# Four edits to a two-layer vision kernel: mixed channels turned by VectorE in the last half, loads ahead of stores at attention's end, one group loaded tile by tile, attention's last sums on TensorE

## The chip, the cores and the metric

The kernel runs on one core of a Trainium2 chip. A core has a matrix engine (TensorE, "PE" in the profile, with its weight loads as "PEld"), a vector engine (VectorE, "DVE"), an activation engine (ScalarE, "ACT"), a general engine (GpSimd, "POOL"), and a synchronizing engine (SyncE, "SP") that here issues every DMA. The DMAs of one queue are spread over 16 DMA engines. Each engine takes its instructions in program order; they wait for each other through semaphores. TensorE writes into PSUM, a small memory of eight banks; everything else lives in SBUF (128 partitions) or in device memory. The metric is the device time of one execution in microseconds.

## The reference

Input x is (2, 56, 56, 384), fp32. Two layers follow each other. Cut to what matters:

```
# layer 0
h = layer_norm(x); q, k, v = heads(h @ w_qkv + b_qkv)        # 12 heads of 32
scores = q . k over each pixel's 7x7 neighbourhood + rpb
x = x + softmax(scores) v @ w_proj + b_proj
x = x + gelu(layer_norm(x) @ w1 + b1) @ w2 + b2              # 384 -> 1536 -> 384
# layer 1
p = layernorm(x) @ w_in + b_in                               # 384 -> 768
local = depthwise_conv_3x3(p)
mixed = 0.25 * (ema(left-right) + ema(right-left) + ema(top-bottom) + ema(bottom-top)) + local
x = x + layernorm(mixed) @ w_out + b_out                     # norm over 768 channels
x = x + gelu(layernorm(x) @ w1 + b1) @ w2 + b2
```

## The kernel before, in words

There are 6,272 tokens (pixels), or 49 tiles of 128. All is fp32; TensorE runs each fp32 product as two passes, so a product of 3 chunks shows as 6 matmul records. A transpose shows as one.

**Attention.** The image is cut into 14 groups of 8 rows (numbers 0 to 13), a group into 4 windows of 14 columns, a window into 3 units of 4 heads: 168 units, `NU`. The loop at L702 makes one step per unit, with the work of several units in each step, in an order that is written out by hand. At step `s` TensorE computes the scores of unit `s` (L515; where two units fit in one bank, both together), VectorE adds the bias in two halves (`biased`, L530), ScalarE takes the exponential (`numerators`, L536), for unit `s-1` VectorE adds up the 2 or 3 chunks of keys into one tile `sum` (`gathered`, L542 and L544), and for unit `s-2` TensorE multiplies the numerators with the values (L552) and `sum` with a matrix of ones (L558), which gives the softmax denominators. The number of chunks `m` depends on the window: 3 in the middle columns of inner groups, 2 at the edges and in the last group. Once a window has its three units, VectorE turns the denominators (`gather`, L482), inverts them (`invert`) and divides (`divide`, L498 and L500).

Beside that, each step may hold a job for TensorE: queries, keys and values of later groups, or `project` (L573), the output projection of one token tile. VectorE then adds the residual `xr` (L585), to which GpSimd has added the bias (`add_bias`, L571). A residual tile is loaded by `load_residual` (L563), which also sets a countdown: after so many steps GpSimd adds the bias, or when the projection needs it, whichever is first. `END` is `ng - 2`, so groups 12 and 13 are the last two: there no later group is prepared any more. At `s == NU` (L736) the memory of keys and biases is freed, the residuals of the last four tiles are loaded and then the first two groups of the attention's output (`xa`, L742, from `x1f`). The stores of finished tiles are issued at the start of each step (`store_all`, L704), and a further residual load (L706) waits until the store of the tile whose buffer it takes has landed. After the loop (L808) come the additions that are left (`take`), the statistics and inverse deviation of the first group (`norm_of`, `close`), its normalization, and the last projections.

**Two passes.** `passes` (L960) then runs over the tokens in groups of 2 or 3 or 4 tiles (`groups`): layer 0's MLP, then layer 1's input projection. Beside it, `Beside` hands out steps of the convolution and the running averages to VectorE; these go over channels on partitions and are stored to `mix_d`. A second loop (L1428) over `dgroups`, eleven groups of 4 tiles, then 3 and 2, runs layer 1's output projection and MLP. In its iteration `g`:

- the hidden loop, 12 times `hidden` (L1053, matmuls L1047): 3 chunks each
- beside it `measure_beside` for group `g + 1`: the mixed channels `mx` have channels on partitions, but the norm over channels wants tokens on partitions, so `measure` (L1246) turns one tile with six TensorE transposes (L1251) into PSUM, and VectorE takes bn_stats of it there (L214). One tile is taken at m = 3, 5, 7 and 9, for the group `half_way` two steps later; `close` follows, whose power runs on GpSimd (L222)
- `project_out` for group `g + 1`: 6 chunks per row of 128 tokens (L1063, `y<-w_out,mx`), and VectorE scales each row by the inverse deviation and adds the residual (L1272)
- the loads of group `g + 2` (`load_mix`, L1233: `mx` from `mix_d`, and `xa`)
- the MLP's second product, 12 chunks per row (L1063, `y<-w,hid`), output additions (L1447) and stores.

The rows of `project_out` and of the second product share two PSUM buffers, `y`. `half_way` is group 6, the first that reaches into the second image; all of VectorE's mixing has to be done before its load, so that is issued at the end of iteration 4 (L1453), after `beside.until`. The last work of `Beside` is thus finished there.

Of the kernel before, what the change touches and what calls it, by code (L numbers as in the profile page):

```python
# [33 lines left out]
F32 = mybir.dt.float32  # L34
# [6 lines left out]
B, H, W, C = 2, 56, 56, 384  # L41
# [132 lines left out]
def block_kernel(ctx: ExitStack, tc: tile.TileContext, ins: dict, out: bass.AP):  # L174
# [328 lines left out]
    class Unit:  # L503
# [33 lines left out]

        def gathered(self):

            n, t = self.w.keys, lp.tile([P, 4, TT], F32, name="sum", bufs=2)  # L540
            self.sum = t
            nc.vector.tensor_tensor(t[:n], self.pts[:n, :, 0, :], self.pts[:n, :, 1, :], ALU.add)  # L542
            for c in range(2, self.m):
                nc.vector.tensor_tensor(t[:n], t[:n], self.pts[:n, :, c, :], ALU.add)  # L544

        def values(self):

            w, hg, n = self.w, self.hg, self.w.keys
            for c in range(self.m):
                for i in range(4):  # L550
                    h = 4 * hg + i
                    nc.tensor.matmul(  # L552
                        o[i * HD : (i + 1) * HD, hg, :],
                        lhsT=w.vt[:n, c, h * HD : (h + 1) * HD], rhs=self.pts[:n, i, c, :],
                        start=c == 0, stop=c == self.m - 1,
                    )
            for i in range(4):
                nc.tensor.matmul(  # L558
                    sums[i * HD : (i + 1) * HD, hg * TT : (hg + 1) * TT], lhsT=ones_hd[:n, :],
                    rhs=self.sum[:n, i, :], start=True, stop=True,  # L560
                )

    def load_residual(t, pool=lp, bufs=3):  # L563

        xrs[t] = pool.tile([P, C], F32, name="xr", bufs=bufs)
        nc.sync.dma_start(out=xrs[t], in_=xf[t * P : (t + 1) * P, :])
        loaded[t] = 4

    def add_bias(t):
        del loaded[t]  # L570
# [30 lines left out]
    def load_group(src, group, tag):  # L601
        t0, n = group
        t = xp.tile([P, NT, C], F32, name=tag)
        nc.sync.dma_start(
            out=t[:, :n, :], in_=src[t0 : t0 + n * P, :].rearrange("(k p) c -> p k c", p=P)
        )
        return t
# [26 lines left out]
    def store_all():  # L634
        while stores:
            dst, src = stores.pop(0)
            nc.sync.dma_start(out=dst, in_=src)
# [63 lines left out]
    END, THEN = ng - 2, (7, 9, 11, 13, 16, 19, 22)  # L701
    for s in range(NU + 4):  # L702
        n, k, hg, i = s // UG, s % UG, s % NC, s // NC
        store_all()  # L704
        while load:
            load_residual(load.pop(0))  # L706
        if k == 0 and n < ng:
            vals = []
            if n + 1 < ng:
                ahead += [lambda n=n, m=m: query_or_key(n + 1, m, one_bank) for m in range(NC)]  # L710
                vals += tiles_of(n + 1)[2:]
            if n + 2 < ng:
                vals += tiles_of(n + 2)[:2]
            ahead += [lambda t=t: value(t, one_bank) for t in vals]
            if n + 2 < ng:
                ahead += [
                    lambda n=n, m=m: query_or_key(n + 2, m, one_bank) for m in range(NC, 2 * NC)
                ]

            spare = (3, 4, 5) if len(ahead) == 9 else (4, 6)  # L720

        if k == 2 and n + 4 < ng:
            load_x(n + 4)
        if k == 1 and n < ng:
            load_bias(n, NWC - 1)
        if n + 1 < ng and k in (4, 10):
            load_bias(n + 1, 0 if k == 4 else 1)
        if s == NU - UG - 4:
            ectx.close()
            wm = ctx.enter_context(tc.tile_pool(name="w_mlp", bufs=1, side="right"))  # L730
            w1, w2, w_parts = weights(0)
        if s < NU and hg == 2 and s + 1 < NU:
            ws[i + 1] = Window(i + 1)
        if s >= NU - UG - 4 and hg == 2 and w_parts:
            w_parts.pop(0)()
        if s == NU:  # L736
            kctx.close()
            xp = ctx.enter_context(tc.tile_pool(name="x", bufs=2, side="right", reuse_waits="tile"))
            tail_pool = actx.enter_context(tc.tile_pool(name="a_tail", bufs=1))
            for t in range(T2 // P - 4, T2 // P):  # L740
                load_residual(t, tail_pool, 4)
            xs = {g: load_group(x1f, groups[g], "xa") for g in range(2)}  # L742


        if s <= NU:
            for take in taking:
                take()
            taking = []
        if s == NU + 1:
            sctx.close()  # L750
            ps_s = sctx.enter_context(tc.tile_pool(name="a_pss", bufs=4, space=PSUM))
        if s < NU:

            if s not in units:
                units[s] = Unit(ws[i], hg)
                units[s].scores()
                behind = Unit(ws[(s + 1) // NC], (s + 1) % NC) if s + 1 < NU else None
                if behind is not None and (units[s].m + behind.m) * TT <= BANK:
                    behind.scores(units[s].m)
                    units[s + 1] = behind  # L760
        new, before, last = units.get(s), units.get(s - 1), units.pop(s - 2, None)
        done = last.w if last is not None and last.hg == NC - 1 else None
        if last is not None:
            last.values()
        behind = ws.get(i - 1 - (hg == 0))
        if behind is not None and hg == 2:
            behind.invert()
        if behind is not None and hg == 0:
            behind.divide()
            if behind.j == NWC - 1:  # L770
                to_project += tiles_of(behind.n)
            ws.pop(behind.i)
        if n + 3 < ng and k < NT:
            measure_x(n + 3, k)
        for half in range(2):
            if new is not None:
                new.biased(half)
                new.numerators(half)
            if half == 0 and done is not None:
                done.take()  # L780
        if before is not None:
            before.gathered()
        if done is not None:
            done.gather()
        if n < END:
            if ahead and k not in spare:
                taking.append(ahead.pop(0)())
            if to_project and n < END - 1:
                taking.append(project(to_project.pop(0), turning_bank))
        elif ahead:  # L790
            if k != 3:
                taking.append(ahead.pop(0)())
        elif s - END * UG in THEN:
            taking.append(project(to_project.pop(0), one_bank))
        elif s > NU and s < NU + 4 and to_project:
            taking.append(project(to_project.pop(0), any_bank))
        for t in list(loaded):
            loaded[t] -= 1
            if loaded[t] < 0:
                add_bias(t)  # L800
        if n + 3 < ng:
            if k in (4, 5):
                for q in range(2 * k - 8, 2 * k - 6):
                    normalize_x(n + 3, q)
            if k in (8, 9, 11):
                taking.append(channels_of(n + 3, (8, 9, 11).index(k), turning_bank))

    for take in taking:  # L808
        take()
    norm = norm_of(xs[0], groups[0][1], sm)  # L810
    norm.close(groups[0][1])
    norm.shift(groups[0][1])
    xn = normalized(norm, xs[0], groups[0][1])
    for t in to_project:
# [145 lines left out]
    def passes(xs, xn, w1, w2, between=lambda psum: None):  # L960
# [272 lines left out]
        def load_mix(g):  # L1233
            t0, n = dgroups[g]
            mx = io.tile([P, NI, MT], F32, name="mx")
            for b, at, here, n in images(t0, n * P):
                nc.sync.dma_start(
                    out=mx[:, :, here : here + n],
                    in_=mix_d[b][:, :, at : at + n].rearrange("m p t -> p m t"),
                )  # L1240
            x = load_group(x2_d, dgroups[g], "xa")
            if g >= half_way:
                add_row(x, dgroups[g][1], "b_out")
            return mx, x, Norm(sm)
# [9 lines left out]
                parts.append(ps.rearrange("p c q -> p (c q)"))  # L1254
            norm.add(k, parts)

        def measure_beside(m, g, ahead, late=0):

            n = dgroups[g][1]
            k = (m - late) // 2 - 1  # L1260
            if m % 2 == 1 and 0 <= k < n:
                measure(ahead[0], ahead[2], k)
            if m == min(10 + late, NHID - 1):
                ahead[2].close(n)

        def project_out(g, mx, x, inner):
# [161 lines left out]
        for g, (t0, n) in enumerate(dgroups):  # L1428
            hid = []
            for m in range(NHID):  # L1430
                hid.append(hidden(w1, m, hT, n, "L1_conv_b1"))
                if g < last:
                    measure_beside(m, g + 1, ahead, 2 if g + 1 == half_way else 0)
                beside.go(MLP_D)
            res = x3
            if g < last:
# [109 lines left out]
```

## Time and profile before

| | us |
|---|---|
| median of 3 runs | 2710.99 (2710.21 to 2712.02) |
| the profiled execution | 2709.48 |
| its span, first to last instruction | 2707.7 |
| busy: TensorE matmul | 2659.7 (98%) |
| busy: VectorE | 1679.7 (62%) |
| busy: ScalarE | 897.7 (33%) |
| busy: GpSimd | 249.6 (9%) |

A matmul's listed duration holds its way through the array, so neighbours overlap, and listed durations add up to more than the time taken; the distance from start to start is what one costs. A group of the profile is one line of the kernel with its engine, operation and tiles. "A <-B" says that the engine stood idle before A until B. `mm`, `y`, `xi`, `o`, `sums`, `sc` and `tp` are PSUM tiles, the others lie in SBUF; names ending in `_d`, `in_...` and `out` are in device memory.

### The profile page before, as it was taken

How to read it: one execution, taken by the hardware profiler on the slowest of the kernel's cores; microseconds unless marked ns; L12 is line 12 of the kernel's file. 1: busy time of each engine (PE TensorE's matmuls, PEld its weight loads, DVE VectorE, ACT ScalarE, POOL GpSimd, SP SyncE). 2: the span in 40 equal slices, each digit the busy share in tenths (PEclk: the TensorE clock that was granted, in tenths of full speed). 3: DMA queues.
4: the chain of work that ended last, by engine and by line, in shares of the span. 5: the costliest groups of instructions: out<-in, count | busy, mean ns of one | idle time of the engine just before them, and what ended most of it. 6: DMA issues, size and time to landing. Idle time of an engine off the chain costs nothing. (4 is left out here: it accounts for less than half of the span.)

```text
span 2707.7 us, 36333 instructions
## 1 busy us (share of the span) xinstructions
PE 2659.7 (98%) x14975; PEld 1492.9 (55%) x14975; DVE 1679.7 (62%) x2560; ACT 897.7 (33%) x1447; POOL 249.6 (9%) x264
## 2 busy tenths in 40 slices
PE   8999999998899999999999999999999999999998
PEld 4666666655555555555554555555555455555565
DVE  3778877878320188688989888898888522221110
ACT  4555555554222332222344422321233211111111
POOL 1111111111211100000010000000100011110100
PEclk9999999999999999999999999999999999999999
DMA  6423454225410132232354544443354411011000
GB/s 213 133 88 104 150 174 149 77 75 167 135 47 27 64 115 79 104 118 98 120 199 183 206 143 141 164 136 117 142 188 171 153 47 44 12 41 35 30 12 16
DMA packets 131887, 298.91 MB, mean 110 GB/s; under 512 B 10646, under 2 KB 87552, under 8 KB 129408
## 3 DMA queue, kind: packets, MB, share of 16 engines
q1 hardware_dynamic: 131712, 296.50, 31.9%
q8 instruction: 119, 1.95, 0.3%
q14 instruction: 56, 0.46, 0.1%
HBM read 180.86 MB, written 115.61 MB: 109 GB/s over the span
## 5 line engine op out<-in xcount | busy, mean ns | idle before, releaser
L1047 PE MATMUL mm<-hT,w 128*128 128x512 f32 (+2 forms) x1872 | 776.1, 570 | 0.1
L1063 PE MATMUL y<-w,hid 128*128 128x384 f32 x2352 | 764.8, 486 | 0.0
L1063 PEld LDWEIGHTS y<-w,hid 128*128 128x128 f32 x2352 | 445.0, 190 | 305.3 <-issue 0.5
L1047 PEld LDWEIGHTS mm<-hT,w 128*128 128x128 f32 x1872 | 352.1, 191 | 372.8 <-issue 342.4
L1056 ACT ACTIVATE hid<-mm,chan 128x512 f32<-128x512 f32 (+2 forms) x312 | 206.3, 662 | 741.2 <-PE mm L1047 741.2
L1141 DVE SCALAR_TENSOR_TENSOR loc<-pt,taps,loc 128x990 f32<-128x990 f32 (+9 forms) x336 | 377.1, 1122 | 10.0 <-ACT loc L1123 1.7
L536 ACT ACTIVATE pts<-pts 119x448 f32<-119x448 f32 (+3 forms) x336 | 206.5, 642 | 187.9 <-DVE pts L530 187.9
L530 DVE TENSOR_TENSOR pts<-sc,bias 119x448 f32<-119x448 f32 (+3 forms) x336 | 220.8, 699 | 67.7 <-PE sc L515 66.7
L222 POOL TENSOR_TENSOR rs<-rs,mhalf 128x4 f32<-128x4 f32 (+4 forms) x67 | 87.2, 1302 | 1745.6 <-DVE rs L219 1704.1
L386 PE MATMUL ps<-hT,wqkv 128*128 128x448 f32 x504 | 211.9, 559 | 3.5 <-ACT vs L431 1.5
L1047 PE MATMUL mm<-hT,w_in 128*128 128x512 f32 (+2 forms) x468 | 191.7, 568 | 0.6 <-ACT hT L254 0.6
L1063 PE MATMUL y<-w_out,mx 128*128 128x384 f32 x588 | 191.8, 486 | 0.0
L1395 DVE TENSOR_TENSOR xc<-y,xa 128x384 f32<-128x384 f32 x49 | 27.3, 557 | 251.0 <-PE y L1063 250.5
L1447 DVE TENSOR_TENSOR xc<-y,xc 128x384 f32<-128x384 f32 x49 | 27.2, 555 | 218.2 <-PE y L1063 167.8
L1063 PEld LDWEIGHTS y<-w_out,mx 128*128 128x128 f32 x588 | 111.6, 190 | 79.8 <-issue 4.8
L240 ACT ACTIVATE xn<-xc,sh,rs 128x384 f32<-128x384 f32 x98 | 64.7, 698 | 269.3 <-DVE sh L233 269.1
L214 DVE BATCH_NORM_STATS2 st<-xi 128x6 f32<-128x384 f32 x98 | 50.3, 554 | 153.3 <-PE xi L1251 153.2
L1047 PEld LDWEIGHTS mm<-hT,w_in 128*128 128x128 f32 x468 | 88.7, 190 | 101.6 <-issue 91.8
L386 PEld LDWEIGHTS ps<-hT,wqkv 128*128 128x128 f32 x504 | 90.2, 191 | 84.4 <-issue 72.8
L254 ACT ACTIVATE hT<-tp,chan 128x512 f32<-128x512 f32 (+2 forms) x117 | 79.5, 751 | 165.1 <-PE tp L251 165.0
L515 PEld LDWEIGHTS sc<-qT,kT 32*100 32x100 f32 (+3 forms) x3168 | 90.9, 169 | 69.5 <-DVE pts L530 17.3
L515 PE MATMUL sc<-qT,kT 32*100 32x112 f32 (+3 forms) x3168 | 113.8, 270 | 9.0 <-DVE pts L530 8.4
(89 smaller groups left out, 2435.4 us busy)
## 6 DMA issues: line engine op xcount, KB each, us to landing
bias<-in_bias_t SPq DMA_DIRECT2D x16, 1344.0 KB
loc<-loc_d SPq DMA_DIRECT2D x24, 784.0 KB
mixed<-mix_d SPq DMA_DIRECT2D x24, 784.0 KB
mix_d<-mixed SPq DMA_DIRECT2D x24, 784.0 KB
xa<-x_d SPq DMA_DIRECT2D x22, 768.0 KB
p_d<-mx SPq DMA_DIRECT2D x10, 1536.0 KB
mx<-mix_d SPq DMA_DIRECT2D x10, 1536.0 KB
pt<-p_d SPq DMA_DIRECT2D x18, 560.0 KB
```

The costliest lines, as they stand in the source:

```text
L214: nc.vector.bn_stats(st[:n, i, :], x)
L222: nc.gpsimd.tensor_tensor(rs, rs, mhalf[:n, :k], ALU.pow)
L240: nc.scalar.activation(out[:, k, :], x[:, k, :], AF.Identity, bias=self.sh[:n, k : k + 1], scale=self.rs[:n, k : k + 1],)
L254: nc.scalar.activation(dst[:, c, : len(xs) * n], tp, AF.Identity, bias=col(b, c), scale=col(g, c))
L386: nc.tensor.matmul(ps, lhsT=wqkv[:, c, m * P : (m + 1) * P], rhs=hT[:, c, half_of(n)], start=c == 0, stop=c == NC - 1,)
L515: nc.tensor.matmul(sc[i // 2][: w.keys, i % 2, (first + c) * TT : (first + c + 1) * TT], lhsT=kT[d, hg, w.keys_at + r * w.kc : w.keys_at + ...
L530: nc.vector.tensor_tensor(self.of(half), sc[half][:n, :, at].rearrange("p h (c q) -> p h c q", q=TT), self.w.bias[:n, 4 * self.hg + h : 4 ...
L536: nc.scalar.activation(self.of(half), self.of(half), AF.Exp)
L1047: nc.tensor.matmul(ps[:, : n * P], lhsT=w[:, c, m * P : (m + 1) * P], rhs=hT[:, c, : n * P], start=c == 0, stop=c == NC - 1,)
L1056: nc.scalar.activation(t[:, : n * P], ps[:, : n * P], AF.Gelu, bias=col(b1, m))
L1063: nc.tensor.matmul(ps, lhsT=t[:, k * P : (k + 1) * P], rhs=w[:, m, :], start=m == 0, stop=m == len(lhs) - 1,)
L1141: nc.vector.scalar_tensor_tensor(to, pt[:, lo + dy - self.top : hi + dy - self.top, xt : xt + n], self.tap(dy, dx), to, ALU.mult, ALU.add,)
```

## The change

Four things are changed.

1. In attention's last two groups (`w.n >= END`) `gathered` adds nothing; TensorE multiplies every chunk of the numerators with the ones, summing in PSUM.
2. At `s == NU` the block that frees memory and loads is moved ahead of `store_all` and the residual loads, `xa` goes ahead of the last four residuals, and these get a countdown of 2 steps instead of 4. After the loop the first group's statistics and `close` go ahead of the waiting `take`s.
3. The load of `mx` for group `half_way` is cut into tiles of 128 tokens (a tile that lies in both images takes two DMAs), and that group is measured at m = 3, 5, 7, 9 like the others, no longer two steps later.
4. For groups after `half_way`, `measure_by_vector` takes the place of `measure`: 16 VectorE transposes per tile, each of 32 partitions and six blocks of 32 columns, into an SBUF tile, and bn_stats from there. It is called at m = 0, 2, 4, 6.

```
         def gathered(self):
-            n, t = self.w.keys, lp.tile([P, 4, TT], F32, name="sum", bufs=2)
-            self.sum = t
+            n, self.parts = self.w.keys, [self.pts[:, :, c, :] for c in range(self.m)]
+            if self.w.n >= END:
+                return
+            t = lp.tile([P, 4, TT], F32, name="sum", bufs=2)
+            self.parts = [t]
             nc.vector.tensor_tensor(t[:n], self.pts[:n, :, 0, :], self.pts[:n, :, 1, :], ALU.add)
...
-            for i in range(4):
-                nc.tensor.matmul(
-                    sums[i * HD : (i + 1) * HD, hg * TT : (hg + 1) * TT], lhsT=ones_hd[:n, :],
-                    rhs=self.sum[:n, i, :], start=True, stop=True,
-                )
+            for c, part in enumerate(self.parts):
+                for i in range(4):
+                    nc.tensor.matmul(
+                        sums[i * HD : (i + 1) * HD, hg * TT : (hg + 1) * TT], lhsT=ones_hd[:n, :],
+                        rhs=part[:n, i, :], start=c == 0, stop=c == len(self.parts) - 1,
+                    )
...
-    def load_residual(t, pool=lp, bufs=3):
+    def load_residual(t, pool=lp, bufs=3, steps=4):
...
-        loaded[t] = 4
+        loaded[t] = steps
...
     for s in range(NU + 4):
         n, k, hg, i = s // UG, s % UG, s % NC, s // NC
+        if s == NU:
+            kctx.close()
+            xp = ctx.enter_context(tc.tile_pool(name="x", bufs=2, side="right", reuse_waits="tile"))
+            tail_pool = actx.enter_context(tc.tile_pool(name="a_tail", bufs=1))
+            xs = {g: load_group(x1f, groups[g], "xa") for g in range(2)}
+            for t in range(T2 // P - 4, T2 // P):
+                load_residual(t, tail_pool, 4, 2)
         store_all()
...
-        if s == NU:
-            kctx.close()
-            xp = ctx.enter_context(tc.tile_pool(name="x", bufs=2, side="right", reuse_waits="tile"))
-            tail_pool = actx.enter_context(tc.tile_pool(name="a_tail", bufs=1))
-            for t in range(T2 // P - 4, T2 // P):
-                load_residual(t, tail_pool, 4)
-            xs = {g: load_group(x1f, groups[g], "xa") for g in range(2)}
...
+    norm = norm_of(xs[0], groups[0][1], sm)
+    norm.close(groups[0][1])
     for take in taking:
         take()
-    norm = norm_of(xs[0], groups[0][1], sm)
-    norm.close(groups[0][1])
     norm.shift(groups[0][1])
...
         def load_mix(g):
             t0, n = dgroups[g]
             mx = io.tile([P, NI, MT], F32, name="mx")
-            for b, at, here, n in images(t0, n * P):
-                nc.sync.dma_start(
-                    out=mx[:, :, here : here + n],
-                    in_=mix_d[b][:, :, at : at + n].rearrange("m p t -> p m t"),
-                )
+            step = P if g == half_way else n * P
+            for t in range(0, n * P, step):
+                for b, at, here, size in images(t0 + t, step):
+                    here += t
+                    nc.sync.dma_start(
+                        out=mx[:, :, here : here + size],
+                        in_=mix_d[b][:, :, at : at + size].rearrange("m p t -> p m t"),
+                    )
...
+        def measure_by_vector(mx, norm, k):
+            t = flat(half("turned", "work"))[:, : NI * P]
+            for i in range(0, P, HD):
+                for j in range(0, P, HD):
+                    nc.vector.transpose(
+                        t[j : j + HD].rearrange("p (m c) -> p m c", m=NI)[:, :, i : i + HD],
+                        mx[i : i + HD, :, k * P + j : k * P + j + HD],
+                    )
+            norm.add(k, [t[:, h * C : (h + 1) * C] for h in range(2)])
+
-        def measure_beside(m, g, ahead, late=0):
+        def measure_beside(m, g, ahead):
             n = dgroups[g][1]
-            k = (m - late) // 2 - 1
-            if m % 2 == 1 and 0 <= k < n:
-                measure(ahead[0], ahead[2], k)
-            if m == min(10 + late, NHID - 1):
+            if g > half_way:
+                if m % 2 == 0 and m // 2 < n:
+                    measure_by_vector(ahead[0], ahead[2], m // 2)
+            elif m % 2 == 1 and 0 < m // 2 <= n:
+                measure(ahead[0], ahead[2], m // 2 - 1)
+            if m == 10:
                 ahead[2].close(n)
...
-                    measure_beside(m, g + 1, ahead, 2 if g + 1 == half_way else 0)
+                    measure_beside(m, g + 1, ahead)
```

## The prediction, written before the changed kernel was run

> **What bounds the kernel now.** I read the busy tenths first, then the groups by line and shape, then TensorE's timeline in the second half, at the half-way point and at attention's end. The page's chain of work is of no use: it holds one 0.56 us addition. The tenths (columns: 40 slices of 67.7 us):
>
> ```profile
> PE   8999999998899999999999999999999999999998
> DVE  3778877878320188688989888898888522221110
> ```
>
> TensorE is full nearly everywhere; VectorE is full until slice 30 and nearly idle after it. So TensorE's own time is what ends the kernel, and three places leave it idle: attention's end (slices 8 to 10), the joint at 701 us, and one wait near 2140 us. Timeline of TensorE, one group of the last half (start, us, engine, line, count):
>
> ```profile
> 2292.76 10.46 PE L1047 MATMUL mm<-hT,w 128*128 128x512 f32 x24
> 2303.06 0.82 PE L1251 MATMUL xi<-ident,mx 128*128 128x128 f32 x6
> 2303.71 5.32 PE L1047 MATMUL mm<-hT,w 128*128 128x512 f32 x12
> ...
> 2326.29 4.03 PE L1063 MATMUL y<-w_out,mx 128*128 128x384 f32 x12
> ```
>
> From start to start, 24 matmuls take 10.30 us, 0.429 us each; six transposes take 0.65 us (2303.06 to 2303.71), far less than six times their listed 276 ns, which overlap. There is no gap. The half-way point and its queue:
>
> ```profile
> 2123.70 15.61 PE L1047 MATMUL mm<-hT,w 128*128 128x512 f32 x36
> 2144.14 1.51 PE L1251 MATMUL xi<-ident,mx 128*128 128x128 f32 x6 [4.83 <-DMA mx<-mix_d]
> 2145.45 6.16 PE L1047 MATMUL mm<-hT,w 128*128 128x512 f32 x12
> ```
>
> ```profile
> 2132.27 1.12 SPq L1226 DMA_DIRECT2D mix_d<-mixed  x2
> 2133.43 2.54 SPq L1237 DMA_DIRECT2D mx<-mix_d  x2
> ```
>
> The load can only follow VectorE's last mixing step (ended 2133.04) and the stores.
>
> Attention's last two groups run from 610 to 687 us (columns: window, length, then busy time and count of PE, PEld, DVE, ACT, POOL, clock, DMA share, GB/s):
>
> ```profile
> 610.00:650.00 40.00, 37.47 (x625) 23.69 (x624) 33.30 (x67) 19.50 (x35) 2.86 (x8) 1.00 0.40 138
> 650.00:687.00 37.00, 27.38 (x539) 17.71 (x537) 31.32 (x69) 14.75 (x30) 7.58 (x13) 1.00 0.66 204
> ```
>
> TensorE is idle there for 2.5 + 9.6 = 12.1 us, mostly waiting for VectorE. The joint after it, timeline:
>
> ```profile
> 693.33 2.23 SPq L566 DMA_DIRECT2D xr<-in_x  x5
> 695.60 0.94 SPq L604 DMA_DIRECT2D xa<-x_d  x2
> ...
> 702.93 0.71 POOL L222 TENSOR_TENSOR rs<-rs,mhalf 128x2 f32<-128x2 f32 x1 [6.12 <-DMA xa<-x_d]
> 703.61 3.85 POOL L571 TENSOR_TENSOR xr<-xr,shift 128x384 f32<-128x384 f32 x4
> ...
> 708.20 1.51 PE L251 MATMUL tp<-ident,xn 128*128 128x128 f32 x6 [7.38 <-DVE bad L820]
> ```
>
> xa lands about 701.1; GpSimd's power and four bias additions follow, VectorE's last addition ends at 708.06, and TensorE goes on.
>
> **What the Trainium skill says.** VectorE: DVE Perf Modes, "Two Vector instructions with no wait between them", gives as a model that a VectorE instruction whose input or output starts in another 32-partition quadrant than the last one's is held until all earlier ones have finished. Each of the 16 new transposes changes its output quadrant, so none overlaps its neighbour. The trace has no such case; it shows the free one (two bn_stats of 554 ns in 1.03 us). The same page, "The three transpose paths", says that this transpose works in 32x32 blocks, which is why 16 are needed. TensorE: Matmul & The Clock Gate, Part 1, says that the array clock falls to half after about 3.4 us of idleness. The trace agrees: the clock record is half for 10.24 us around the 7.38 us gap and for 3.41 us around the 4.83 us gap. DMA: Bandwidth & Descriptors, "Specifications", asks for 512 B or more per transfer; here 256 B packets took 18 ns and 1,792 B packets 78 ns, so small ones move 14 instead of 23 B/ns.
>
> **The change part by part.**
>
> *VectorE turns (groups after half way).* These are groups 7 to 12 of the last part: 4+4+4+4+3+2 = 21 tiles. TensorE loses 21 x 6 transposes: 21 x 0.655 = 13.8 us, all of it on its own path. VectorE gets 16 transposes of 32x192 per tile. The nearest rows:
>
> ```profile
> L214 DVE BATCH_NORM_STATS2 st<-xi 128x6 f32<-128x384 f32 x98 | 50.3, 554 | 153.3 <-PE xi L1251 153.2
> ...
> L482 DVE STREAM_TRANSPOSE turned<-sums 128x352 f32<-128x352 f32 x56 | 30.5, 544 | 8.8 <-PE sums L558 8.8
> ```
>
> VectorE's slope is 1.04 ns an element (L1141: 730 ns for 495, 1,244 for 990), so 352 elements are 0.366 us and 0.175 us is fixed. 192 elements are 0.20 + 0.175 = 0.375 us; held, with the 0.03 us from one VectorE instruction to a dependent one, 0.41. Bounds: 0.25 if they overlap after all, 0.60 if short runs cost. A tile: 16 x 0.41 + 1.03 + 0.24 for the aggregate = 7.8 us; four tiles 31.3 us.
>
> What covers it: the first turn queues behind the last output addition (0.7 us into the group's hidden loop). Statistics then end at 32.0; closing 0.16, power 1.0 and two handovers make 33.4. The hidden loop without transposes is 72 x 0.429 = 30.9 us, the first projected row ends 3.9 us later (12 x 0.323), at 34.8: the inverse deviation is there first. TensorE would wait only when the third row finds both y buffers full, at 38.7, and an eviction takes 0.62: 4.3 to 4.7 us of cover. Behind the turns on VectorE are the close and the projected rows' evictions, and for these TensorE waits. So nothing is paid while a transpose is below 0.48 us. Three tiles (beside a loop of four) and two (beside 23.3 us) have more room. mx is needed at m = 0 instead of 3; the next one is issued a whole group ahead and landed by 2151, needed at 2211. Value: -13.8.
>
> *Sums on TensorE (groups 12 and 13 of attention).* Twelve units at two chunks in the last group, six of two and six of three before: 30 VectorE additions go, 30 x 0.62 = 18.6 us. TensorE gets 30 x 8 matmuls. What eight cost, on the timeline:
>
> ```profile
> 685.10 0.37 PE L558 MATMUL sums<-sum,ones_hd 102*32 102x112 f32 x8
> 685.19 0.42 PEld L552 LDWEIGHTS o<-pts,vt 102*32 102x32 f32 x16
> 685.29 0.57 PE L552 MATMUL o<-pts,vt 102*32 102x112 f32 x16
> ```
>
> 0.19 us, so 5.7 us. With 12.1 us idle, TensorE can't shorten the stretch by more than 12.1 - 5.7 = 6.4; if VectorE's relief were worth nothing it would lose 5.7. In 610 to 650 TensorE is nearly the bound already; in 650 to 687 VectorE is, but TensorE also waits there up to 1.0 us at a time for vt, whose loads stand in SP's queue behind residual loads that wait for a store to land (up to 8.6 us), beside 204 GB/s. I take half: -3.
>
> *Loads ahead of stores.* xa (960 KB) and four residuals (768 KB) move on SP ahead of the store of tile 41, which SP issued at 688.36, and so ahead of the residual of tile 44, which waits for that store. xa can land some 5 us sooner. But the store now issues about 3 us later behind 1.7 MB of loads, and tile 44's residual lands last, near 702.5. In the new order its addition stands on VectorE ahead of the shift that xn needs, then two activations and four evictions: TensorE restarts near 706.5 to 707.5 where it did at 708.2. The four bias additions on GpSimd move ahead of the power (countdown 2), so they are no longer last. Bounds: 4 if the residual is early, +1.5 if late. Value: -1.5.
>
> *Half way, tile by tile and two steps earlier.* The first turn comes after 24 matmuls, at 2134.0, not after 36. Its tile now needs two loads of 768 packets of 256 B each (768 of them took 0.95 us before, so 1.9 us), begun at 2138.0 where the stores' data end, landing with the last engine's lag (1 us before) near 2140.9. The wait is then 6.9 us, not 4.8. In the profile, 36 matmuls and four turns (18.1 us) from 2144.14 would end at 2162.2, and did at 2163.7: 1.5 us went to the half clock. Now, from 2141.0, 48 matmuls and four turns (23.2 us) and the same loss make 2165.7. The later tiles (768 packets of 512 B, about 1.4 us each) are on time. Value: +2, between 0 and +5.
>
> Sum: -13.8 - 3 - 1.5 + 2 = -16.3. The profiled execution took 2709.48 us (span 2707.7 and 1.8 around it), so 2693.2; the median of the runs is 1.5 above it: 2694.7.
>
> **Rivals.** *Attention's end stays with the loads*: the sums free VectorE, and the same TensorE waits go over to vt and the residuals, while the longer wait at half way costs 5. For it: DMA share 0.66; against it: VectorE at 31.3 of 37 us. -13.8 + 5 = -8.8: 2702.2.
> *Attention's end packs*: TensorE falls to its own work (-6.4), the joint gives 4, half way costs nothing more than 0.5. -23.7: 2687.3. Against it: the vt waits.
> *VectorE becomes the bound (slower)*: if the turn of short runs takes 0.65 us, four tiles overrun the cover by 64 x (0.65 - 0.477) = 11 us in each of four groups and 6 in the next, 50 in all: net +34, 2745. It decides from about 0.54 us, where overrun equals the 16.3 gained. For it: strided VectorE reads are dear elsewhere (L1215, 868 ns for 392). Against it: here the inner 32 elements are contiguous.
> *The transposes' time isn't freed*: if something else paced the loop, 2709. Against it: 0.65 us between matmul starts, in all 21 places.
>
> **How the numbers follow.** Likeliest (all four parts with these signs) 0.64, own range 2688 to 2701; loads 0.14; packed 0.11; VectorE's overrun 0.08; not freed 0.03. Faster 0.64 + 0.14 + 0.11 = 0.89, within 0.2% (5.4 us, about what can be told from no change) 0.03, slower 0.08. The range 2686 to 2704 takes in the first three but their edges and leaves out the last two.
>
> **What would show it.** In the last half, no L1251 and about 336 VectorE transposes at 0.35 to 0.45 us with starts as far apart; no TensorE gap ahead of the projected rows. At half way a wait of 6 to 8 us. Between 610 and 687, VectorE 18 us less busy, the stretch 2 to 5 us shorter. A turn above 0.48 us, or a TensorE wait at y, makes the prediction wrong.

## The result, and the profile after

The changed kernel takes 2697.91 us (median of 6, 2696.13 to 2702.19) where the kernel before takes 2711.15; the ratio is 0.9954, 95% interval 0.9941 to 0.9967. That is 13.2 us faster where 16.3 was forecast (2694.7), and inside the range of 2686 to 2704. The profiled execution took 2697.28 us, its span 2695.5.

Tenths of busy time of the changed kernel, 40 slices of 67.4 us:

```profile
PE   8999999999999999999999999999999899999998
DVE  3778877876320098688989888898888534555430
```

VectorE, which had 5 2 2 2 2 1 1 1 0 in the last nine slices, now has 5 3 4 5 5 5 4 3 0. Groups by line and shape of the changed kernel (line, engine, operation, tiles, shape, count, busy us, mean ns, idle time before and its releaser):

```profile
L1271 DVE STREAM_TRANSPOSE turned<-mx 32x192 f32<-32x192 f32 x336 | 123.3, 367 | 4.2
...
L1260 PE MATMUL xi<-ident,mx 128*128 128x128 f32 x168 | 23.6, 278 | 7.3 <-DMA mx<-mix_d 7.3
...
L214 DVE BATCH_NORM_STATS2 st<-turned 128x6 f32<-128x384 f32 x42 | 21.4, 552 | 0.7
```

336 turns are 21 tiles of 16, and 126 of the 294 TensorE transposes are gone; of the 168 that stay, the first of group 6 waits 7.3 us. TensorE and then VectorE in the first group of the last half, on the timeline (start, us, engine, line, count):

```profile
2212.39 31.06 PE L1052 MATMUL mm<-hT,w 128*128 128x512 f32 x72
2243.29 15.64 PE L1068 MATMUL y<-w_out,mx 128*128 128x384 f32 x48
```

```profile
2213.07 6.10 DVE L1271 STREAM_TRANSPOSE turned<-mx 32x192 f32<-32x192 f32 x16
2219.20 1.02 DVE L214 BATCH_NORM_STATS2 st<-turned 128x6 f32<-128x384 f32 x2
2220.25 0.21 DVE L215 BATCH_NORM_AGGREGATE mv<-st 128x2 f32<-128x12 f32 x1
2220.38 6.06 DVE L1271 STREAM_TRANSPOSE turned<-mx 32x192 f32<-32x192 f32 x16
...
2242.32 0.16 DVE L219 SCALAR_TENSOR_TENSOR rs<-mv,ones 128x4 f32<-128x4 f32 x1
2247.43 0.62 DVE L1295 SCALAR_TENSOR_TENSOR xc<-y,rs,xa 128x384 f32<-128x384 f32 x1 [4.94 <-PE y L1068]
```

The 72 hidden matmuls run through and the 48 of the projection follow at once. A tile takes VectorE 7.3 us, four of them 29.3, and it still stands idle for 4.94 us ahead of the first projected row: covered.

Half way, TensorE:

```profile
2121.10 10.46 PE L1052 MATMUL mm<-hT,w 128*128 128x512 f32 x24
2138.87 1.51 PE L1260 MATMUL xi<-ident,mx 128*128 128x128 f32 x6 [7.31 <-DMA mx<-mix_d]
2140.18 7.20 PE L1052 MATMUL mm<-hT,w 128*128 128x512 f32 x12
...
2164.64 15.64 PE L1068 MATMUL y<-w_out,mx 128*128 128x384 f32 x48
```

The wait has grown from 4.83 to 7.31 us, and twelve matmuls take 7.03 us from start to start after it instead of 5.15: the record of the clock granted to TensorE is at half up to 2143.96. Attention's last groups, windows (length, then busy time and count of PE, PEld, DVE, ACT, POOL, clock, DMA share, GB/s):

```profile
610.00:650.00 40.00, 39.16 (x750) 26.10 (x749) 24.20 (x50) 19.59 (x35) 2.84 (x8) 1.00 0.40 137
650.00:687.00 37.00, 31.05 (x570) 21.47 (x569) 22.32 (x52) 13.37 (x27) 7.28 (x13) 0.91 0.61 189
```

VectorE has lost 18.1 us of work here, as meant, but TensorE has filled up from 37.47 to 39.16 of 40 us in the first window, and the stretch is no shorter. The joint:

```profile
691.25 1.01 SPq L609 DMA_DIRECT2D xa<-x_d  x2
...
700.62 0.33 SPq L571 DMA_DIRECT2D xr<-in_x  x1
...
703.21 0.99 POOL L576 TENSOR_TENSOR xr<-xr,shift 128x384 f32<-128x384 f32 x1
704.24 0.56 DVE L590 TENSOR_TENSOR xr<-ps,xr 128x384 f32<-128x384 f32 x1 [5.24 <-POOL xr L576]
704.71 0.15 DVE L233 SCALAR_TENSOR_TENSOR sh<-mv,rs 128x2 f32<-128x2 f32 x1
...
704.85 2.20 PE L582 MATMUL ps<-wproj,og 128*128 128x384 f32 x6 [2.12 <-DVE xr L590]
...
707.80 0.84 PE L251 MATMUL tp<-ident,xn 128*128 128x128 f32 x6 [0.74 <-DVE bad L825]
```

xa is issued at 691.25 and no longer the last: tile 44's residual is, issued at 700.62 once its store has landed; its bias addition ends at 704.2, and only then come VectorE's addition and the shift, and the row that TensorE waits for. TensorE restarts at 707.80 instead of 708.20, but its longest wait ahead of that is now 2.12 us, where it was 7.38.

Both profiles cut at the same events (first exponential of units 0, 144, where group 12 begins, and 167, the last; the first transposes of the passes; the hidden loop and the first projected row half way; TensorE's last row; the end), lengths in us:

| from, to | before | after | difference |
|---|---|---|---|
| start, unit 0 | 50.37 | 48.54 | -1.8 |
| unit 0, unit 144 | 561.32 | 562.86 | +1.5 |
| unit 144, unit 167 | 72.43 | 76.09 | +3.7 |
| unit 167, restart | 24.08 | 20.31 | -3.8 |
| restart, half way | 1415.50 | 1413.30 | -2.2 |
| half way, its first row | 40.02 | 43.54 | +3.5 |
| first row, last row done | 536.75 | 522.94 | -13.8 |
| tail | 7.2 | 7.9 | +0.7 |

The first two rows are not the change's: nothing is edited there. The first is how soon the first loads arrive; the second is one window at half clock more (6.83 us near 584 us, where before had 3.41).

With the experiments below there are 14 profiles, and in many of them the code of a row is the same. This shows what one profile says of a row. From the first row to the last, all nine with the turns (each turn done once) agree to 0.02 us, and so do all four without; 13.8 us lie between. But from unit 144 to the restart three kernels with the code of before take 95.3 to 97.5 us, and five with the changed kernel's code 94.4 to 98.9: there, a difference of 2 us between two profiles shows nothing.

### The profile page after: what moved, and what is told of

It reads as the page before. It is cut to its first block, busy times and chain, and to the rows that moved or that the text cites. A ratio compares the mean times of both kernels' runs of the same rounds, so it can differ in the third digit from the quotient of the medians.

```text
span 2695.5 us, 36876 instructions
## 1 busy us (share of the span) xinstructions
PE 2654.6 (98%) x15089; PEld 1487.6 (55%) x15089; DVE 1784.0 (66%) x2866; ACT 897.4 (33%) x1447; POOL 249.4 (9%) x264
## 5 line engine op out<-in xcount | busy, mean ns | idle before, releaser
L1271 DVE STREAM_TRANSPOSE turned<-mx 32x192 f32<-32x192 f32 x336 | 123.3, 367 | 4.2
```

The lines of the kernel that those rows point to most:

```text
L1271: nc.vector.transpose(t[j : j + HD].rearrange("p (m c) -> p m c", m=NI)[:, :, i : i + HD], mx[i : i + HD, :, k * P + j : k * P + j + HD],)
```

## The experiments

The theory after the comparison (A): the turns gave all the gain; the sums bought nothing, because TensorE was full in group 12 and waits for loads (`vt`) in group 13; the joint gained through the clock; half way lost through a longer wait. The rival (B): the parts have the sizes that the prediction gave them, and the rest is chance.

### One part at a time

`turn_only`, the kernel before with part 4 alone:

```
+            if g > half_way:
+                if m % 2 == 0 and m // 2 < n:
+                    measure_by_vector(ahead[0], ahead[2], m // 2)
             k = (m - late) // 2 - 1
-            if m % 2 == 1 and 0 <= k < n:
+            if g <= half_way and m % 2 == 1 and 0 <= k < n:
```

> Only the VectorE turns of the groups after half way; the rest is as before. If the 126 TensorE transposes were on the path and the turns are covered, 21 x 0.655 = 13.8 us go: about 2697.3. If a part of the gain came from the other edits, it is less than 12 us. No TensorE wait ahead of the projected rows in either case.

2696.88 us against 2710.83, ratio 0.9952 (0.9939 to 0.9966): 14.0 us by the medians. The turns alone give as much as all four edits, and TensorE waits ahead of none of the projected rows.

`sums_only`, part 1 alone:

```
+            if self.w.n >= END:
+                return
...
+            for c, part in enumerate(self.parts):
```

> Only the sums on TensorE in groups 12 and 13. Theory A (TensorE is already full in group 12, and in group 13 it waits for vt, whose loads stand in SP's queue behind a residual load that waits for a store): VectorE's relief buys nothing and the 5.7 us of added matmuls cost, so +1 to +4 us by unit 167, and the time 0 to +4 us. Rival B (VectorE paces, as the prediction had it; the later unit 167 in the changed kernel's profile is a half-clock accident): -3 us.

2711.92 us, ratio 1.0009 (1.0000 to 1.0017): no gain, and by the medians a loss of 1.1 us. B's -3 is out. Group 12 shows where it is lost: from unit 144 to unit 156, where group 13 begins, takes 42.63 us in each of the eight profiles with the sums on TensorE, and 41.47 or 41.48 in each of the six without. The 18 chunks added there cost some 3.4 us of TensorE (an estimate, at the prediction's 0.19 us each), while its waits for the biased scores (`pts`) from VectorE only fall from 3.5 us to 1.7. TensorE of this kernel in group 13:

```profile
667.42 0.40 PE L556 MATMUL o<-pts,vt 120*32 120x112 f32 x8 [2.15 <-DMA vt<-v_d]
668.48 0.40 PE L556 MATMUL o<-pts,vt 120*32 120x112 f32 x8 [0.66 <-DMA vt<-v_d]
```

Its six waits for vt come to 7.0 us (2.15, 0.66, 1.26, 1.07, 0.95, 0.89), where the kernel before had 3.4 us in five. This difference can't be put down to the edit. With the code of before there, `half_only` shows 1.0 us and `turn_only` 4.7; with the changed kernel's code, `no_half` shows none and `one_quadrant` 5.4. From unit 156 to unit 167 the profiles with the sums take 30.7 to 34.8 us, those without 30.9 to 35.4. So no gain shows in group 13 either, and what holds it is not shown.

`loads_only`, part 2 alone:

> Only the reordered loads at the joint. Theory A: TensorE restarts about 0.5 to 1.5 us sooner than in the kernel before, and has no full idle window there, so the 10.24 us at half clock go too (2.7 us): -2 to -4 us in all. Rival B: tile 44's residual is as late as xa was, and nothing is won: within 1 us of before.

```
+        if s == NU:
+            kctx.close()
...
+            xs = {g: load_group(x1f, groups[g], "xa") for g in range(2)}
+            for t in range(T2 // P - 4, T2 // P):
+                load_residual(t, tail_pool, 4, 2)
         store_all()
```

2705.84 us, ratio 0.9984 (0.9977 to 0.9990): 5.0 us by the medians. In its profile, from unit 167 to the restart takes 20.65 us, 3.4 less than before. Group 13 ahead of it, where nothing is edited, takes 2.0 more, with the clock at half for 6.83 us, so from unit 144 to the restart only 1.5 are left (95.03). From the restart to the next common wait (TensorE's short one ahead of the first input projection) it takes 763.56 us instead of 765.75. In between there is no edit: these 2.2 us are the clock, whose record has no half window after this restart, where before had one up to 713.55. The other profiles agree: from the restart to half way, all ten with part 2 take 1413.3 us and have no half window there; the four without take 1415.1 to 1416.0, each with one.

`half_only`, part 3 alone:

```
+            step = P if g == half_way else n * P
...
-                    measure_beside(m, g + 1, ahead, 2 if g + 1 == half_way else 0)
+                    measure_beside(m, g + 1, ahead)
```

> Only the tile-wise load and the earlier turns at half way. Theory A: TensorE comes to the first turn 5 us sooner, the first tile lands 2 to 3 us sooner than the whole did, so the wait is about 7.3 us and the time +3 to +5 us with the longer half clock. Rival B (the prediction's size): +2. Rival C (smaller first load is worth what it was made for): -1 to -3.

2714.25 us, ratio 1.0013 (1.0007 to 1.0020): 3.4 us slower by the medians (1.9 to 5.4), at the same place:

```profile
2122.67 10.46 PE L1047 MATMUL mm<-hT,w 128*128 128x512 f32 x24
2140.47 1.51 PE L1255 MATMUL xi<-ident,mx 128*128 128x128 f32 x6 [7.33 <-DMA mx<-mix_d]
```

Over all profiles, from half way to the first row takes 42.2 to 44.0 us in the six with part 3 and 40.0 to 41.5 in the five that load and turn as before.

The four medians add up to -13.95 + 1.1 - 5.0 + 3.4 = -14.5; together they give -13.2.

### Half way: is it the turns' place or the packets?

`no_half` undoes part 3 in the changed kernel; `tiles_late` undoes only its second half, and keeps the tile-wise load:

```
-        def measure_beside(m, g, ahead):
+        def measure_beside(m, g, ahead, late=0):
...
+            k = (m - late) // 2 - 1
+            if g <= half_way and m % 2 == 1 and 0 <= k < n:
+                measure(ahead[0], ahead[2], k)
+            if m == min(10 + late, NHID - 1):
```

> The changed kernel with the half-way group loaded and turned as before. Theory A (the half-way edit costs by its 2.5 us longer wait and a second window at half clock): 3 to 4 us below the changed kernel, about 2694. Rival: if the edits lean on each other, the same as the changed kernel, 2698.

> The changed kernel with the tile-wise load kept, but the half-way turns two steps later, as before. Theory A: the first tile lands some 17.8 us into the hidden loop and TensorE asks for it after 36 matmuls, 15.45 us, so it waits about 2.3 us, and no whole window is idle; from the loop's start to the first projected row 36 to 37 us, where the kernel before had 40.0 and the changed one 43.5: about 2691. Rival B (smaller packets are what makes the load late): the wait stays near 5 us and the time at 2694 or more.

`no_half` has 2692.84 us, ratio 0.9940 (0.9923 to 0.9956), `tiles_late` 2691.61, ratio 0.9935 (0.9919 to 0.9952), beside 2708.82 for the kernel before. The two times can't be told apart; the traces can. Timeline of `tiles_late`:

```profile
2122.51 15.61 PE L1052 MATMUL mm<-hT,w 128*128 128x512 f32 x36
2140.30 0.85 PE L1260 MATMUL xi<-ident,mx 128*128 128x128 f32 x6 [2.18 <-DMA mx<-mix_d]
```

Asked for after 36 matmuls, the first tile keeps TensorE waiting 2.18 us; it is there 17.8 us into the loop, as in the changed kernel (2138.87 - 2121.10). So the tile-wise load is sooner than the whole one by 2.7 us (20.4 before), and the turns at m = 3 threw that away. One half-clock window of 3.41 us still followed, so 37.6 us to the first row, not the 36 to 37 expected; `no_half` takes 41.2.

### Attention's end: the order of loads

`vt_first`, the changed kernel with one move:

```
+        if END <= n and s < NU - 1 and hg == 2:
+            ws[i + 1] = Window(i + 1)
         store_all()
...
-        if s < NU and hg == 2 and s + 1 < NU:
+        if n < END and hg == 2 and s + 1 < NU:
```

> The changed kernel with the vt loads of groups 12 and 13 issued ahead of the step's stores and residual loads. Theory A (in group 13 TensorE waits for vt because the load stands behind a residual that waits for a store to land): TensorE's three vt waits (3.5 us) go and unit 167 comes 3 to 6 us sooner against unit 144, the time 2 to 4 us below the changed kernel. Rival B (the DMA engines are full there, so the order doesn't matter): the waits stay, within 1 us of the changed kernel.

2697.88 us, ratio 0.9956 (0.9940 to 0.9973): as the changed kernel. But the move changes SP's queue in one place only. The first vt loads of group 13 now go out at 645.17, ahead of a residual load behind which they stood in the changed kernel (650.52); the other three pairs still stand behind residual loads, which an earlier step had issued:

```profile
659.71 0.33 SPq L571 DMA_DIRECT2D xr<-in_x  x1
660.40 0.33 SPq L316 DMA_DIRECT2D bias<-in_bias_t  x1
660.83 1.52 SPq L465 DMA_DIRECT2D vt<-v_d  x2
...
672.39 0.33 SPq L571 DMA_DIRECT2D xr<-in_x  x1
672.77 1.50 SPq L465 DMA_DIRECT2D vt<-v_d  x2
```

The waits for vt are gone from TensorE's timeline, but they are gone from that of `no_half` too, which has the changed kernel's order; from unit 156 to unit 167 the two take 31.91 and 31.89 us. So theory A's cause of the vt waits is not tested by this run, and what these waits cost stays open.

`tail_five` gives tile 44 a buffer of its own, loaded with the last four:

```
-            if t + 3 < T2 // P - 4:
+            if t + 3 < T2 // P - 5:
...
+            for t in range(T2 // P - 5, T2 // P):
+                load_residual(t, tail_pool, 5, 2)
```

> The changed kernel with the residual of tile 44 loaded with the last four, in a buffer of its own, instead of behind the store whose buffer it took. Theory A (what ends last at the joint is tile 44: its load waits for a store, and VectorE's addition stands ahead of the shift and of the rows that TensorE needs buffers from): the 2.1 us wait of TensorE ahead of a projection goes and the restart comes 2 to 4 us sooner: about 2695. Rival B (GpSimd's four additions and the power set the restart): within 1 us of the changed kernel.

2694.88 us, ratio 0.9939 (0.9922 to 0.9955), where the changed kernel has 0.9954. The joint in its profile:

```profile
698.54 6.07 PE L582 MATMUL ps<-wproj,og 128*128 128x384 f32 x18 [0.47 <-DVE xr L590]
...
703.57 0.71 POOL L222 TENSOR_TENSOR rs<-rs,mhalf 128x2 f32<-128x2 f32 x1
704.31 0.16 DVE L233 SCALAR_TENSOR_TENSOR sh<-mv,rs 128x2 f32<-128x2 f32 x1 [3.93 <-POOL rs L222]
704.39 1.94 DVE L590 TENSOR_TENSOR xr<-ps,xr 128x384 f32<-128x384 f32 x4
...
706.48 0.85 PE L251 MATMUL tp<-ident,xn 128*128 128x128 f32 x6 [1.86 <-DVE bad L825]
```

The wait of 2.1 us ahead of a projection, which all six profiles with the changed kernel's order show (2.1 to 2.2 us), is gone; the restart itself now waits 1.86 us where it waited 0.74. The next thing late is GpSimd's power, which now stands behind five bias additions, with VectorE's shift and the last four additions behind it. By the medians 3.0 us are gained, but the two intervals overlap; from unit 144 to the restart 94.3 us lie at the edge of the scatter of the changed kernel's code (94.4 in `more_turns`).

### What a turn costs, and where its cover ends

`one_quadrant`, the changed kernel with each turn written into the quadrant (32 partitions) from which it is read, which leaves the turned channels out of their places:

```
-                        t[j : j + HD].rearrange("p (m c) -> p m c", m=NI)[:, :, i : i + HD],
+                        t[i : i + HD, j * NI : (j + HD) * NI].rearrange("p (m c) -> p m c", m=NI),
```

> The changed kernel with each VectorE transpose writing into the quadrant that it reads, four in a row in one quadrant and into separate columns; the turned channels are thus not in their places and the deviations come from misplaced values. Same count, same size. Theory A (a change of quadrant holds the next instruction, which makes 0.382 us from start to start): 12 of 16 starts follow after about 0.25 us, a tile's turns take some 4.5 us instead of 6.1. Rival B (this operation never overlaps itself): 0.38 us as before. The time is the changed kernel's in both cases, since the turns are covered.

Its VectorE timeline, against 6.06 and 6.10 us in the changed kernel:

```profile
2212.47 4.63 DVE L1271 STREAM_TRANSPOSE turned<-mx 32x192 f32<-32x192 f32 x16
2217.13 1.02 DVE L214 BATCH_NORM_STATS2 st<-turned 128x6 f32<-128x384 f32 x2
```

Within a quadrant the next turn starts after 0.26 us while the last is still running (0.32 us listed); where the quadrant changes it takes 0.34 us, the whole duration and 0.015. In the changed kernel, where every turn changes its output quadrant, every start is 0.38 us after the last. So the rule of the Trainium skill, VectorE: DVE Perf Modes, "Two Vector instructions with no wait between them", that an instruction which changes quadrant starts only when the earlier ones have finished, holds here, in both directions. (The edit also writes the columns side by side, and a turn lists 0.32 us instead of 0.37; that part is not the quadrant's.) The time, 2696.7 us in a single run, is the changed kernel's: 1.5 us per tile less on VectorE buy nothing.

`more_turns` does eight of the 16 turns twice:

```
-            for i in range(0, P, HD):
+            for i in (*range(0, P, HD), 0, HD):
```

> The changed kernel with eight of the 16 turns of each tile done twice, so that VectorE works longer on nothing new. A tile took 7.28 us from first turn to first turn; 8 x 0.382 more make 10.3, four of them 41.4. Theory (the cover ends at 38.7 us after the group's first matmul, when both y buffers are full): with 0.7 us ahead and 2.2 us of close, power, handovers and eviction, TensorE waits about 5.5 us ahead of the third projected row in each of four groups and not in the one of three tiles: 22 us, with half-clock windows 26 to 32, about 2725. Rival (VectorE's work in the last half is hidden whatever it is): 2698.

2733.47 us, ratio 1.0086 (1.0069 to 1.0103), 35.6 us above the changed kernel. Its TensorE:

```profile
2209.61 31.06 PE L1052 MATMUL mm<-hT,w 128*128 128x512 f32 x72
2240.51 7.90 PE L1068 MATMUL y<-w_out,mx 128*128 128x384 f32 x24
2254.91 11.07 PE L1068 MATMUL y<-w_out,mx 128*128 128x384 f32 x24 [6.50 <-DVE xc L1295]
```

Two projected rows go through, the third waits 6.50 us for a y buffer, as the prediction's slower rival had it; so in each of four groups (6.57, 6.57 and 6.56), 26.2 us, and none in the group of three tiles. The other 9.4 us go with the half clock (the record has 6.8 to 10.2 us at half beside each wait). The wait is 1 us longer than expected: a tile costs 10.62 us here, not 10.3.

### Put together

`best_a` drops the sums from the changed kernel, takes `tail_five`, and turns group 6 at m = 6, 8, 10 and 11; `best_b` adds the move of `vt_first`.

```
+            elif g == half_way:
+                if m in (6, 8, 10, 11):
+                    measure(ahead[0], ahead[2], (6, 8, 10, 11).index(m))
```

> The changed kernel without the sums on TensorE, with tile 44 loaded as in tail_five, and the half-way turns at m = 6, 8, 10 and 11 of a tile-wise load. If the parts add up: -14 for the turns, -5 for the loads, -2 to -4 for tile 44, and at half way no wait (TensorE asks after 42 matmuls, 18.0 us into the loop, and the first tile lands at 17.8), 33.6 us to the first projected row where the kernel before had 40.0, so -6: about 2683. If attention's end takes the gain at the joint back (it lost 3 us in the profile with loads alone), 2686.

> best_a with the vt loads of groups 12 and 13 ahead of stores and residual loads. Without the sums on TensorE, VectorE paces these groups, and TensorE's vt waits (3.4 us in the kernel before) are partly beside VectorE's work: 0 to 3 us below best_a.

`best_a` has 2684.86 us, ratio 0.9901 (0.9884 to 0.9918), `best_b` 2684.35, ratio 0.9898 (0.9882 to 0.9915): both beat both kernels, and each other by nothing that can be told. Neither waits for vt in group 13. Half way in `best_a`:

```profile
2119.17 18.19 PE L1047 MATMUL mm<-hT,w 128*128 128x512 f32 x42
2137.20 0.82 PE L1255 MATMUL xi<-ident,mx 128*128 128x128 f32 x6
```

No wait, and no half clock: 33.5 us to the first row. From unit 144 to the restart `best_a` takes 94.4 us and `best_b` 94.2, although unit 167 comes after 76.9 and 75.3.

## Why the prediction was right, point by point

*The bound.* TensorE's time sets the end: the part that took work from it gave its price in full, and adding work to VectorE cost nothing until TensorE had to wait.

*VectorE turns, -13.8.* Right in mechanism and size: -13.8 between the first and last row of the changed profile, -14.0 alone. The turn was taken at 0.41 us and cost 0.38, the tile at 7.8 and cost 7.3; that it would be held was right. The cover was said to end at 38.7 us, with two full y buffers; `more_turns` shows that end.

*Sums on TensorE, -3.* Wrong in sign: +1.1 alone. The step that failed is "I take half". The bound from both sides (6.4 us to be won, 5.7 to be lost) was right, and the text itself held the fact that decides in group 12, TensorE nearly full in 610 to 650 (now 39.16 of 40): there the sums cost 1.16 us in every profile that has them. In group 13, where the half was to be won, nothing is won that stands out of the scatter. The text named the vt waits as the rival there; whether they are the cause is not shown. One of its own signs, a stretch 2 to 5 us shorter, did not come: from unit 144 to the restart it is 96.4 us after and 96.5 before.

*Loads ahead of stores, -1.5.* Right in sign, too small: 5.0 by the medians (2.7 to 6.2). Tile 44's residual became the last, as worked out, but from unit 167 to the restart the part alone saved 3.4 us. And a term was missing: with TensorE's idle time at the joint cut into pieces, the half clock after it went, 2.2 us. The clock rule was quoted ahead of this and used only half way.

*Half way, +2.* Right in sign and mechanism: +3.4 alone, with 2 just inside its interval of 1.9 to 5.4. The wait was put at 6.9 us and was 6.5 to 7.3 in the six profiles. "And the same loss" to the half clock was too little: the clock was at half for 6.83 or 10.24 us there, in the five profiles without the part for 3.41 or 6.83.

In sum -13.8 + 1.1 - 5.0 + 3.4 = -14.3 against -16.3 forecast and -13.2 measured: errors of +4, -3.5 and +1.4 that partly cancelled. The turns were forecast; that the three small parts together came so near is luck.

## What to carry to other kernels

Work moved off a full engine pays its price in start-to-start time, as long as the receiving engine finishes before the last buffer behind it fills; that moment can be worked out from the page and is worth testing by adding work. Where two limits stand close together, relief of one can be worth nothing, so halving a bound is no estimate: ask, stage by stage, which limit is next. And move the point at which a load is asked for together with the load: a tile that comes 2.7 us sooner is no use to a consumer that asks 5 us sooner. Before you explain a difference between two profiles, see how far profiles with the same code in that stretch differ. And see in the trace whether a move in the code has moved the queue.

## What the runs showed of the hardware

- TensorE's clock falls to half without a long gap: in `vt_first` no gap in attention's end ahead of it exceeds 1.4 us, and a projection of six matmuls lists 3.56 us where 2.20 is usual, at a half window from 657.41 to 660.82. The kernel before shows the same from 587.26 to 590.67, with no gap above 1.2 us ahead. The rule of the Trainium skill that the prediction quotes (TensorE: Matmul & The Clock Gate, Part 1), half clock after about 3.4 us of idleness, is thus not the whole of it.
- In each of the 14 traces (the clock's record begins some 14 us into the span) the half windows start on one grid of 3.41 us and last 3.41, 6.83 or 10.24 us, but for the last, which the end cuts. By the listed times, TensorE was busy for at most 62% of the grid window ahead of each such stretch; after no busier window did one begin, and after windows of 45 to 61% not always. So executions of the same code differ by which stretch falls into a window: up to unit 144 by 1.5 us, with nothing edited there.
- Within a quadrant a 32x192 VectorE transpose follows the last after 0.26 us, across quadrants after its whole 0.34 to 0.38 us.
- Half way, packets of 256 B took 18 ns each, of 512 B 34 and of 1,792 B 78. Although its packets were smaller, the first tile was there 2.7 us sooner than the whole load.
